# Patch loads of 16 rows plus two single rows, and patch writes issued on GpSimd, in a two-layer convolution by learned codes

## The chip, the cores and the metric

The kernel runs on one core of a Trainium2 chip. The metric is the device time of one execution in microseconds (us). A lower time is better.

## The reference, cut to what matters

The input is 16 images of 256 channels and 28x28 pixels. After a group norm, two layers of the same kind follow. In each, every channel's 3x3 patch (9 values) is compared with 16 codes; the softmax of the distances weights a table lookup, and the lookups are summed over channels.

```python
def amm_conv3x3(x, centroids, w_sub, stride=1):
    patches = jax.lax.conv_general_dilated_patches(x, (3, 3), (stride, stride), 'SAME')
    p = patches.reshape(B, C, s, Ho * Wo).transpose(0, 3, 1, 2)
    d = sum(p * p) - 2.0 * einsum('bncs,cks->bnck', p, centroids) + sum(centroids * centroids)
    attn = jax.nn.softmax(-d, axis=-1)                 # over the 16 codes
    lut = jnp.einsum('cks,cso->cko', centroids, w_sub)
    out = jnp.einsum('bnck,cko->bno', attn, lut)
    ...
# x + relu(se_layer(bn(amm(relu(bn(amm(gn(x))))))) + gn(x))
```

## The kernel before

The program is a plan of 32 stages (one layer of one image each) with 16 slots to a stage. A slot handles one unit: 32 channels and half of the pixels. From stage 2 to stage 28 the even stages are layer 2, and from stage 3 to stage 27 the odd ones are layer 1. Three kinds of transfers matter here, and they are issued by two engines.

```python
    def to_pat(l, i, pat, px=0, n=HW):          # patch WRITE, 12 per stage, used two stages later
        ...
        nc.scalar.dma_start(
            view(pat, (ROWS * p0 + 9 * k + 3 * dx) * HW + px, [[ROWS * HW, m], [HW, 3], [1, n]]),
            bass.AP(v.tensor, v.offset, [list(v.ap[0]), [W, 3], [1, n]]),
        )

    def patches(u, tile):                       # patch LOAD, four transfers of 18 rows
        ...
        for i in range(4):
            nc.sync.dma_start(
                pt[32 * i : 32 * i + ROWS, :, :n],
                view(u["pat"], (16 * u["m"] + i) * ROWS * HW + px, [[HW, ROWS], [4 * ROWS * HW, 4], [1, n]]),
            )

    def m_out(u):                               # maxima of a unit out to memory: two transfers
        for p0, n in ((0, P), (P, 96)):
            nc.scalar.dma_start(view(d, 32 * p0, [[32, n], [256 * 32, 4], [1, 32]]), u["mt"][:n])

    def m_in(u):                                # ... and back as extra rows of the patch tile: two transfers
        for j in range(NCH):
            nc.scalar.dma_start(u["pt"][MROW + j :: 32, :, :n], view(u["dm"], ...))
```

The round trip `m_out`, `m_in` through the buffer `dm` is made by two of the eight units in each pixel half of layer 2, so four times in a stage. The plan puts it behind an early pass of logits:

```python
                    if m in maxed:
                        a = s - self.lb                      # lb = 6 slots before the unit's own slot
                        self.loads.append((a - self.lead, s, u))   # lead = 3
                        at(a, MAX, a_logits, u)
                        ...
                        at(a + 2, TURN_BACK, m_turn, u)
                        at(a + 3, TURN, m_out, u)
                        at(a + 4, TURN, m_in, u)
                    else:
                        self.loads.append((s - self.lead, s, u))
                    at(s, LOGITS, b_logits, u)
                    at(s, EXP, b_exp, u)
    ...
    LOGITS, EXP, LOOK_A, NUM, TURN, SMALL, LOOK_B, MAX, LOOK_C, TURN_BACK, LOAD, REST = range(12)
```

## Time and profile before

| | before |
|---|---|
| time, median of 2 runs | 3104.32 us (3103.53 to 3105.12) |
| span of the profiled run | 3103.0 us |
| start to the first numerators | 54.8 us |
| stages 0 and 1 | 250.7 us |
| 13 layer-1 stages (3, 5, ..., 27) | 1257.8 us, mean 96.8 |
| 14 layer-2 stages (2, 4, ..., 28) | 1235.4 us, mean 88.2 |
| stages 29 to 31 and the end | 304.2 us |

A stage is timed from its first group of numerator matmuls to the first of the next stage, and a slot in the same way, so that a slot's time holds its own early logits (`a_logits`) and the next slot's logits (`b_logits`). The five rows of time add up to the span. The page of the profile has, further, the DMA queues (packets, megabytes, share of all 16 DMA engines' time) and the chain of work that ended last:

```profile
q10 hardware_dynamic: 151488, 244.45, 31.5%
q1 hardware_dynamic: 180560, 241.14, 30.6%
q0 software_dynamic: 6912, 38.54, 4.2%
PE 76%; DMA 10%; DVE 5%; POOL 3%; issue 2%; ACT 2%; ACTq 1%; SPq 0%; POOLq 0%; DVEq 0%
```

`q1` is SyncE's queue with the loads, `q10` is ScalarE's with the writes and the round trips, and `q0` is GpSimd's. The DMA engines are occupied for about two thirds of the span; a tenth of the last chain is transfers. TensorE carries three quarters of that chain.

### The profile page before, as it was taken

What the parts mean: (1) busy time and instruction counts of PE and PEld (TensorE: products, weight loads), DVE (VectorE), ACT (ScalarE), POOL (GpSimd) and SP (SyncE); (2) the same over time, 40 slices, a digit from 0 to 9 for tenths busy, and PEclk for the clock granted to TensorE, in tenths of its full rate; (3) what the DMA queues carried; (4) which work ended last, traced back from release to release, by engine and by line L of the source; (5) the groups of instructions that cost most, each with busy time, mean ns of one, the idle gap of its engine ahead of it and who ended that gap; (6) DMA issues with size and microseconds to landing.
All of it is one profiled execution on the core that took longest, in us unless ns stands there. A gap on an engine that the chain in (4) does not pass through costs nothing.

```text
span 3103.0 us, 94273 instructions
## 1 busy us (share of the span) xinstructions
PE 2966.8 (96%) x39834; PEld 1165.8 (38%) x39834; DVE 2254.3 (73%) x2760; ACT 1094.8 (35%) x1605; POOL 1506.4 (49%) x2163
## 2 busy tenths in 40 slices
PE   4998999999999999999999999999999999999997
PEld 3432333333333333333333333333333433334333
DVE  3464777777777777777777787777777777777785
ACT  2331342433434233342433334243343423333332
POOL 2352454555545455464545545455453545546444
PEclk8998999999999999999999999999999999999998
DMA  7866777767757676675767767676775767664552
GB/s 204 215 148 133 202 201 188 190 163 190 187 148 188 148 202 169 182 183 146 192 158 199 182 165 184 157 194 156 192 187 144 193 148 202 171 170 114 146 136 58
DMA packets 339391, 530.25 MB, mean 171 GB/s; under 512 B 94240, under 2 KB 265488, under 8 KB 338960
## 3 DMA queue, kind: packets, MB, share of 16 engines
q10 hardware_dynamic: 151488, 244.45, 31.5%
q1 hardware_dynamic: 180560, 241.14, 30.6%
q0 software_dynamic: 6912, 38.54, 4.2%
q8 instruction: 316, 5.18, 0.7%
q14 instruction: 115, 0.94, 0.1%
HBM read 269.96 MB, written 254.05 MB: 169 GB/s over the span
## 4 chain that ended last, share of the span: by engine, by line
PE 76%; DMA 10%; DVE 5%; POOL 3%; issue 2%; ACT 2%; ACTq 1%; SPq 0%; POOLq 0%; DVEq 0%
PE acc L695 45%; PE pair L631 15%; PE pair L563 15%; DMA pt<-pat 6%; DMA pat<-side 3%; DVE nt L643 2%; POOL k L659 1%; DVE rc L649 1%; ACT e L621 1%; DVE q L677 1%; POOL total L671 1%; DMA pat<-im 1%; ACTq L468 1%; PE pair L324 1%; DVE gn_st L417 0%
## 5 line engine op out<-in xcount | busy, mean ns | idle before, releaser
L695 PE MATMUL acc<-q,ws 128*128 128x384 f32 (+1 forms) x4096 | 1662.5, 525 | 5.3 <-ACT y L717 5.3
L659 POOL TENSOR_TENSOR k<-nt,rc 128x832 f32<-128x832 f32 (+1 forms) x512 | 804.8, 1572 | 1538.5 <-DVE rc L649 1527.1
L643 DVE STREAM_TRANSPOSE nt<-pair 128x832 f32<-128x832 f32 (+1 forms) x1024 | 977.4, 993 | 765.3 <-PE pair L631 640.7
L621 ACT ACTIVATE e<-pair 128x800 f32<-128x800 f32 (+1 forms) x1024 | 787.3, 821 | 1499.7 <-PE pair L563 1308.7
L695 PEld LDWEIGHTS acc<-q,ws 128*128 128x128 f32 x4096 | 705.1, 191 | 922.5 <-issue 610.0
L563 PE MATMUL pair<-pt,wd 19*32 19x384 f32 (+2 forms) x18432 | 626.5, 509 | 60.5 <-DMA pt<-pat 58.6
L631 PE MATMUL pair<-e,cw 32*32 32x384 f32 (+1 forms) x16384 | 585.9, 507 | 14.5 <-ACT e L621 13.3
L677 DVE STREAM_TRANSPOSE q<-k 128x832 f32<-128x832 f32 (+1 forms) x512 | 489.2, 956 | 0.8 <-POOL k L659 0.8
L649 DVE RECIPROCAL rc<-nt 128x104 f32<-128x104 f32 (+1 forms) x512 | 398.6, 779 | 17.6
L563 PEld LDWEIGHTS pair<-pt,wd 19*32 19x32 f32 (+1 forms) x18432 | 149.3, 103 | 440.6 <-issue 265.6
L631 PEld LDWEIGHTS pair<-e,cw 32*32 32x32 f32 x16384 | 167.2, 104 | 360.5 <-ACT e L621 317.9
L665 POOL TENSOR_TENSOR tail<-nt,rc 128x104 f32<-128x104 f32 (+1 forms) x512 | 245.1, 479 | 0.0
L695 PE MATMUL acc<-qt,ws 128*128 128x400 f32 (+1 forms) x512 | 218.8, 509 | 0.0
L671 POOL TENSOR_TENSOR total<-total,nt 128x96 f32<-128x96 f32 (+1 forms) x448 | 200.3, 447 | 0.0
L671 POOL TENSOR_TENSOR total<-total,rc 128x96 f32<-128x96 f32 (+1 forms) x448 | 179.1, 400 | 0.0
L695 PEld LDWEIGHTS acc<-qt,ws 128*128 128x128 f32 x512 | 91.0, 190 | 100.8 <-issue 51.3
L587 DVE TENSOR_REDUCE mx<-z 128x48 f32<-128x768 f32 (+1 forms) x128 | 120.8, 944 | 0.0
L582 DVE STREAM_TRANSPOSE z<-pair 128x768 f32<-128x768 f32 (+1 forms) x128 | 119.4, 971 | 1.8 <-PE pair L563 1.8
L707 ACT ACTIVATE im<-acc,bnsh,bnsc 128x384 f32<-128x384 f32 (+1 forms) x64 | 43.4, 678 | 137.0 <-PE acc L695 135.2
L717 ACT ACTIVATE y<-acc,bnsh,bnsc 128x384 f32<-128x384 f32 (+1 forms) x64 | 43.4, 679 | 88.7 <-PE acc L695 79.5
L525 DVE SCALAR_TENSOR_TENSOR y<-xt,gn_rstd,y 128x392 f32<-128x392 f32 x64 | 71.2, 1116 | 1.2 <-ACT y L519 1.2
L533 POOL TENSOR_TENSOR y<-y,xt 128x392 f32<-128x392 f32 x64 | 64.8, 1015 | 11.0 <-ACT y L529 11.0
(104 smaller groups left out, 620.7 us busy)
## 6 DMA issues: line engine op xcount, KB each, us to landing
pat<-side ACTq DMA_DIRECT2D x232, 588.0 KB
pt<-pat SPq DMA_DIRECT2D x1024, 112.5 KB
pt<-pat SPq DMA_DIRECT2D x1024, 108.0 KB
pat<-im ACTq DMA_DIRECT2D x116, 588.0 KB
xt<-in_x POOLq DMA_DIRECT2D x32, 784.0 KB, 8.7
out_dram<-y POOLq DMA_DIRECT2D x16, 784.0 KB, 6.4
pat<-side ACTq DMA_DIRECT2D x24, 300.0 KB
pat<-side ACTq DMA_DIRECT2D x24, 288.0 KB
```

Of the source, the lines that this page charges most:

```text
L563: nc.tensor.matmul(ps[t // 2][c : c + 32, t % 2, :n], lhsT=wd[l][32 * i : 32 * i + rows, 4 * u["m"] + t, :], rhs=u["pt"][32 * i : 32 * i + ...
L582: nc.vector.transpose(z[:, : 64 * nb].rearrange("p (t m) -> p t m", t=2), ps[:, :, : 32 * nb])
L587: nc.vector.tensor_reduce(u["mx"][:, 2 * v : 2 * v + 2].rearrange("p t (j b) -> p t b j", j=2)[:, :, :nb], u["z"].pop(0)[:, : 64 * nb].rea ...
L621: nc.scalar.activation(e[:, :, :n], ps[:, :, :n], AF.Exp, scale=2.0)
L631: nc.tensor.matmul(u["nm"][t // 2][32 * i : 32 * i + 32, t % 2, :n], lhsT=cw[l][c : c + 32, 4 * u["m"] + t, :], rhs=es[t // 2][c : c + 32, ...
L643: nc.vector.transpose(nt[:, :nb, 2 * v : 2 * v + 2].rearrange("p b t r -> p t b r"), ps[:, :, : 32 * nb].rearrange("p t (b r) -> p t b r", ...
L649: nc.vector.reciprocal(rc[:, : 8 * nb], u["nt"][:, :, SUM])
L659: nc.gpsimd.tensor_tensor(q[:, :nb].rearrange("p b (a s) -> p (b a) s", s=8), nt[:, :, :8], rc.unsqueeze(2).to_broadcast([P, 8 * nb, 8]), ...
L665: nc.gpsimd.tensor_tensor(tails[key][:, :nb, 8 * (m % 4) : 8 * (m % 4) + 8], nt[:, :, 8].rearrange("p (b a) -> p b a", a=8), rc.rearrange( ...
L671: nc.gpsimd.tensor_add(t[:, : 8 * nb], t[:, : 8 * nb], v)
L677: nc.vector.transpose(q[:, :, : 32 * nb].rearrange("p h (b r) -> p h b r", r=32), u.pop("k")[:, :nb].rearrange("p b (h r) -> p h b r", h=2),)
L695: nc.tensor.matmul(accs[key][:, :n], lhsT=ws[l][:, 2 * m + h if h < 2 else 2 * NQ + m // 4, o * P : (o + 1) * P], rhs=u["q"][h][:, :n], st ...
```

## The change

The intent is to have a load use all 16 DMA engines instead of nine, and to take the patch writes out of the way of the loads by another issuing engine. The load is also moved to an earlier place in each slot.

```diff
     def to_pat(l, i, pat, px=0, n=HW):
...
-        nc.scalar.dma_start(
+        nc.gpsimd.dma_start(
...
         for i in range(4):
             nc.sync.dma_start(
-                pt[32 * i : 32 * i + ROWS, :, :n],
-                view(u["pat"], (16 * u["m"] + i) * ROWS * HW + px, [[HW, ROWS], [4 * ROWS * HW, 4], [1, n]]),
+                pt[32 * i : 32 * i + 16, :, :n],
+                view(u["pat"], (16 * u["m"] + i) * ROWS * HW + px, [[HW, 16], [4 * ROWS * HW, 4], [1, n]]),
+            )
+        for r in range(16, ROWS):
+            nc.sync.dma_start(
+                pt[r::32, :, :n],
+                view(u["pat"], (16 * u["m"] * ROWS + r) * HW + px, [[ROWS * HW, 4], [4 * ROWS * HW, 4], [1, n]]),
             )
...
-    LOGITS, EXP, LOOK_A, NUM, TURN, SMALL, LOOK_B, MAX, LOOK_C, TURN_BACK, LOAD, REST = range(12)
+    LOGITS, LOAD, EXP, LOOK_A, NUM, TURN, SMALL, LOOK_B, MAX, LOOK_C, TURN_BACK, REST = range(12)
```

The matmuls and all arithmetic stay the same. A load has six transfers for four.

## The prediction

> **What bounds the kernel now.** I read the busy table first, then who TensorE (PE) waited for, then the same waits by stage, and last the queue of SyncE (SP), which issues the patch loads. The program is a row of 32 stages (layer 1 or layer 2 of one image) of 16 slots each. A slot is one unit: 16 small logits matmuls on a patch tile `pt` (L563), exp on ScalarE, 16 small numerator matmuls (L631), transposes, a scale on GpSimd, and some nine accumulating matmuls (L695).
>
> ```profile
> PE 2966.8 (96%) x39834; PEld 1165.8 (38%) x39834; DVE 2254.3 (73%) x2760; ACT 1094.8 (35%) x1605; POOL 1506.4 (49%) x2163
> PE pair L563 <- DMA pt<-pat: 58.6, 39, 4.9
> ```
>
> PE is busy 96%, so the whole idle time is 136 us, and nearly all of it in mid-program is the logits waiting for a patch load (58.6 us in 39 waits). Other engines are far from full. So the question is what these waits cost in all, and whether the change removes them. The stretches below are stage 15 (layer 1), stage 16 (layer 2) and stage 29 (the last layer-1 stage); columns are length, busy time of each engine (instructions), granted clock, DMA share, GB/s.
>
> ```profile
> 1506.80:1603.00 96.20, 92.48 (x1249) 35.62 (x1248) 69.09 (x82) 37.08 (x56) 51.12 (x77) 0.96 0.72 178
> 1603.00:1690.50 87.50, 87.50 (x1241) 34.62 (x1240) 70.76 (x88) 30.57 (x44) 42.61 (x60) 1.00 0.67 175
> 2798.80:2885.50 86.70, 86.70 (x1244) 34.55 (x1243) 69.24 (x82) 32.37 (x49) 49.55 (x70) 1.00 0.48 113
> ```
>
> A layer-1 stage takes 96.2 us, with 3.7 us of PE idle time and a mean clock of 0.96; a layer-2 stage has the same matmuls, no idle time, and takes 87.5. Stage 29 is a control that the program makes by itself: layer 1 again, but no patch writes beside it, since no later stage needs them; it takes 86.7. Taking slot by slot (start of one L631 group to the next), stage 15 loses all of it in slot 14: 15.3 us, against 7.8 in slot 14 of stage 29. The same slot takes 14.6 to 16.0 us in twelve of the thirteen layer-1 stages 3, 5, ..., 27 (11.1 in the other). In the timeline of PE it looks like this:
>
> ```profile
> 1585.46 0.93 PE L563 MATMUL pair<-pt,wd 19*32 19x384 f32 x32
> ...
> 1589.77 0.83 PE L563 MATMUL pair<-pt,wd 19*32 19x400 f32 x2 [1.84 <-DMA pt<-pat]
> 1591.79 3.41 PE L563 MATMUL pair<-pt,wd 19*32 19x400 f32 x30 [1.20 <-DMA pt<-pat]
> 1595.13 3.04 PE L695 MATMUL acc<-q,ws 128*128 128x400 f32 x4
> ```
>
> Two waits of 1.84 and 1.20 us; then 32 logits instructions take some 5.4 us where they took 0.93, as the row tiles land one by one; then four L695 matmuls take 3.04 us, normally 1.61. The clock records say why: half speed for 6.8 us from 1591.5. So a stall of 3 to 4 us costs 7 to 8. Over stages 2 to 30 I sum 55 us idle and 92 us at half clock.
>
> Why is the load late? SP's own queue:
>
> ```profile
> SPq L550 <- DMA pat<-side: 650.6, 180, 14.0
> SPq L550 <- DMA pat<-im: 404.4, 63, 15.1
> SPq L550 <- DMA pt<-pat: 378.1, 491, 4.6
> SPq L550 <- DMA dm<-mt: 304.6, 55, 21.4
> ```
>
> No load here reads a patch that is still being written: the writes (`pat<-side`, `pat<-im`, issued by ScalarE) are for a stage two later. The instruction records show the reason: loads and ScalarE's DMAs signal on the same eight semaphores in turn (108, 110 to 116), and SP waits for a semaphore's earlier transfer to land before using it again. At 1580.23 ScalarE issued a write on semaphore 115; the late load wanted 115 and was issued at 1586.70; SP had stood still since 1578.9. So 1055 us of SP's waits are false waits for patch writes.
>
> Second cause, the DMA engines. By packet size the trace has 150,624 load packets of 1536 or 1600 bytes, mean 96 ns, and about nine 4-byte completion packets per load (19,680 on that queue for some 2,150 DMAs). In stage 15, 9 or 10 load packets are in flight for 35 of 97 us and 11 or more for only 7: a load runs on nine engines.
>
> **What the Trainium skill says.** "DMA: Bandwidth & Descriptors", § Why a DMA increments its semaphore by 16 and not by 1: the number of engines is the largest k up to 16 that divides the slowest dimension of both sides. 18 rows give 9, which agrees with the trace; 16 rows would give 16, and the four-row transfers 4 (the lowest-numbered). The same page, § Issuing engines are not separate DMA queues: another issuer only saves issue time, so moving the writes to GpSimd frees no bandwidth; what I expect from it is the semaphores, which that section doesn't treat. § SWDGE vs HWDGE vs iDMA: GpSimd's descriptors are computed by software on its own cores. The trace: 0.75 to 0.81 us of GpSimd time per 256-row DMA, 0.58 us of queue time for ScalarE's. "TensorE: Matmul & The Clock Gate", Part 1: the clock falls to half after an idle window of about 3.4 us and needs a busy one to recover; the 6.8 us (two windows) agree.
>
> **The change part by part.**
>
> *Writes on GpSimd* (420 issues). GpSimd's DMAs use semaphores of their own (107 for its store), so SP's 1055 us of waits on writes go. Cost: 420 x 0.75 us (from the 0.75 to 0.81 of the larger `xt` and `out_dram` DMAs) = 315 us on GpSimd, 1506 to about 1820 us, 59%. It stands idle 1527 us waiting for `rc`; its result is used three slots later, so 0.75 us per slot lies beside other work. ScalarE loses 420 x 0.59 = 250 us of queue time, which is worth nothing to PE (13 us of waits for `e`).
>
> *16 + two single rows.* Engines 0 to 3 carry 16 + 8 = 24 packets per load, the rest 16, where nine carried 32. A layer-1 stage has 18 loads (two units' loads fall early): nine engines x 18 x 32 x 96 ns = 55 us each. Its other traffic: 0.72 x 16 x 96 = 1108 us of engine time, less 500 for loads (18 x 288 x 96 ns), over 16 = 38 us each. So those nine have 93 of 96 us full: layer 1 is bound by them too, and the lag builds up until slot 14. After: 18 x 24 x 96 ns = 41 + 38 = 79 us of 88 on four engines, 28 + 38 = 66 on the others. Tight, not full. Cost on SP: six issues for four, at 0.27 to 0.59 us (SP's range for shapes of this size): at most 3.5 us per 5.5 us slot.
>
> *Loads right behind the logits.* SP runs by itself, so this only changes whose semaphore a load gets in turn: it now stands before the slot's `dm` transfers. Worth 0 to 1 us per stage.
>
> Sum, stage by stage. Layer-1 stages 3 to 27 take 1257.8 us (13); with slot 14 at 7.5 and the other slots at their usual values one is 88.2, 1146.6 in all: 111 saved at most; I allow 1 us left in each: 98. Layer-2 stages 2 to 28 have 13 us over 14 x 87.3: 6 saved. Stage 30 (97.9, slot 6 takes 13.2 for about 7.3): 5. Stage 1 (125.9, loads behind small weight moves on SP, which stay): 8. Less 3 for unforeseen waits: 3104 - 114 = 2990 us.
>
> **Rivals.** (1) *The four single-row engines become the bound.* 79 of 88 us is an average; slot 11 has two loads, a patch write and the 784 KB store. If half the stall stays, PE may still idle a whole window: some 50 us saved, 3050. Against: SP can now run ahead by the spare tiles. (2) *The dm round trip takes its place.* ScalarE's `m_out` and `m_in` still share the eight semaphores, and SP waited 304.6 us on `dm<-mt`, 21 us at once. With six DMAs per load, eight semaphores span only 1.3 loads. But stage 30 and layer-2 stages have the same trips and mostly no stall, and `m_out` no longer queues behind writes: 3010 if it bites. (3) *GpSimd becomes late* by waiting in order for ScalarE's shifts, or by descriptor work: against it, 49% busy and three slots of slack; it would show 3060 or more. (4) *Everything hidden anyway*: against it, stage 29.
>
> **Range and chances.** The most that I can find is about 140 us (111 + 13 + 10 + some of stage 1), so 2962 is the low end; rival 1 in full gives the high end, 3045. The 2% line is 3042. Faster 0.85, same 0.12, slower 0.03.
>
> **What would show it.** PE's wait for `pt<-pat` falls from 58.6 us to under 15; layer-1 stages take 87 to 90 us, clock 1.00; SP's waits on `pat<-side` and `pat<-im` vanish; GpSimd gains 420 DMAs and some 300 us of busy time, without PE waiting on it; the load queue's share of the engines stays near 30%. I am wrong if slot 14 still takes over 11 us, if L695 starts to wait on `q`, or if a GpSimd-issued write slows the loads beside it.

## The result, and the profile after

The changed kernel takes 3491.82 us (3482.81 and 3500.82 in two runs), against 3104.32: a ratio of 1.1248, interval 1.1123 to 1.1374. It is slower by an eighth. A ratio is the mean time of one kernel's fast runs over the mean of the other's in the same rounds, so it is not quite the ratio of the two medians.

Line numbers move by six: the logits are now L569, the numerators L637, the lookup matmuls L701; the 16-row transfers are issued at L551 and the single rows at L556. The busy line of the changed kernel:

```profile
PE 3031.8 (87%) x39834; PEld 1185.9 (34%) x39834; DVE 2257.0 (65%) x2760; ACT 1096.5 (31%) x1605; POOL 1765.2 (50%) x2583
```

The instruction count of TensorE is the same, but it is busy 65 us longer (3031.8 for 2966.8) and idle 467 us (3498.9 - 3031.8) where it was 136. So 331 of the 396 us are idle time and 65 are matmuls at a lower clock. GpSimd has its 420 more instructions, and these cost what was foreseen:

```profile
L468 POOL DMA_DIRECT2D pat<-side x280 | 186.1, 665 | 5.1 <-DMA pt<-pat 4.3
L468 POOL DMA_DIRECT2D pat<-im x140 | 93.8, 670 | 2.7 <-ACT im L447 2.6
```

The columns are busy time, mean ns of one, and the idle time before: 280 us of issue, 0.67 us each. No wait of TensorE is for GpSimd's scale; one of 12.5 us, in the setup, is for GpSimd's squares (3.0 before). What TensorE does wait for (in all, times, longest):

```profile
PE pair L569 <- DMA pt<-pat: 265.8, 82, 7.4
PE pair L569 <- issue: 98.4, 22, 6.8
```

The wait that should have fallen from 58.6 us to under 15 rose to 265.8. (The second line is at the logits too. This view says "issue" where the last releaser came more than 1 us before the start; in 18 of the 22 waits that releaser was a load, `pt<-pat`, which had landed 1 to 3 us earlier. What held the logits from there on is not shown.) The chain that ended last has 52% TensorE for 76%, and 25% transfers for 10%:

```profile
PE 52%; DMA 25%; DVE 9%; issue 5%; POOL 4%; SPq 2%; ACT 1%; ACTq 1%; DVEq 0%; POOLq 0%
```

And the queue of SyncE, which issues the loads:

```profile
SPq L551 <- DMA dm<-mt: 436.3, 32, 17.6
SPq L556 <- DMA dm<-mt: 393.8, 44, 15.0
```

This is the view to compare with the one of before. The two lines for `pat<-side` and `pat<-im`, 1055 us together, are gone but for 15 us, as intended. In their place `dm<-mt`, which is `m_out`, went from 304.6 us to 436.3 + 393.8 = 830.1 us. No load reads `dm`; this is a false wait again, with another holder.

Where in the program the time went, stage by stage:

| | before | after | difference |
|---|---|---|---|
| start to the first numerators | 54.8 | 59.1 | +4.3 |
| stages 0 and 1 | 250.7 | 250.3 | -0.4 |
| 13 layer-1 stages | 1257.8 | 1294.7 | +36.9 |
| 14 layer-2 stages | 1235.4 | 1551.9 | +316.5 |
| stages 29 to 31 and the end | 304.2 | 343.0 | +38.8 |

Four fifths of the loss lie in the layer-2 stages, which by the prediction were to gain 6 us. Stage 15, stage 16 and stage 29 of the changed kernel answer to the three stretches that the prediction shows (length, busy time of each engine, granted clock, DMA share, GB/s):

```profile
1697.70:1797.50 99.80, 91.72 (x1245) 35.67 (x1244) 69.30 (x82) 37.05 (x56) 59.07 (x89) 0.93 0.78 175
1797.50:1906.30 108.80, 93.42 (x1237) 36.05 (x1236) 70.79 (x87) 30.79 (x44) 49.34 (x71) 0.92 0.65 137
3155.90:3247.50 91.60, 87.97 (x1243) 34.86 (x1242) 69.20 (x82) 32.32 (x49) 49.96 (x71) 0.98 0.56 115
```

Stage 16 takes 108.8 us for 87.5, with 15 us of idle TensorE where there was none, and the clock falls to 0.92. Stage 29, which has no patch write beside it (but for one in its first microsecond in the changed kernel, some 70 us before the stall) but does have the `m_out` of the stage behind it, went from 86.7 to 91.6, all of it in slot 14 (12.6 us for 7.8). That alone says that what is new does not need a patch write.

Slot by slot, the loss of the layer-2 stages sits in three places: slot 2 takes 11.6 us for 7.5, slot 6 takes 16.7 for 7.6, and slot 10 takes 12.9 for 4.8. In layer 1 slot 14 takes 18.4 for 14.8. These are the slots just behind an `m_out`. The timeline shows one of them, at the end of stage 15 (start, length, engine, and in brackets the idle time before and its releaser):

```profile
1770.00 1.91 ACTq L608 DMA_DIRECT2D dm<-mt  x2
...
1773.47 0.30 SPq L551 DMA_DIRECT2D pt<-pat  x1
...
1775.49 0.83 PE L701 MATMUL acc<-q,ws 128*128 128x400 f32 x2
1776.41 2.73 SPq L556 DMA_DIRECT2D pt<-pat  x2
1776.49 2.68 ACTq L614 DMA_DIRECT2D pt<-dm  x2
1779.24 2.07 SPq L551 DMA_DIRECT2D pt<-pat  x4
...
1782.39 1.60 PE L569 MATMUL pair<-pt,wd 19*32 19x384 f32 x32 [6.07 <-DMA pt<-pat]
```

ScalarE issues the two transfers of `m_out` from 1770.00 on. By the semaphore records they land at 1773.41 and 1776.40. SyncE issues one load transfer at 1773.47, on the semaphore of the first, and then stands still until 1776.41, when the second has landed and its semaphore is free. What is left of the load are the two single rows; the second takes 2.14 us to issue and lands at 1782.35. TensorE has run out of work at about 1776.3 and waits 6.07 us for the load. The 32 logits after it take 1.60 us instead of 0.93, since the granted clock is at half from 1778.7 on.

The theory from this, called A: SyncE's loads and ScalarE's transfers take turns on the same eight completion semaphores, and a transfer waits until the earlier one on its semaphore has landed. With the writes gone from ScalarE, the only other users are the round trips; and with six transfers to a load, eight semaphores come round faster, so that a load meets an `m_out` that has only just been issued. I counted this in the programs as built, where every transfer names its semaphore. In stages 3 to 27, this many load transfers have an `m_out` as the last user of their semaphore:

| | one slot ahead of the load's use | two slots | four slots | behind a patch write |
|---|---|---|---|---|
| before | 0 | 46 | 12 | 214 |
| after | 50 | 12 | 0 | 0 |

In the changed kernel the 50 are for the logits of slot 14 (26), 2 (12) and 6 (12), and the 12 at two slots are all for slot 11, whose logits lie in the time of slot 10: these are the four places that stall.

The turns are not those of the plan: a load that the plan places ahead of an `m_out` may take its turn behind it. They can be read off the built program all the same. In every one of these programs the transfers of SyncE and ScalarE together take the eight semaphores in strict rotation, in the order in which the built program lists them (2,835 transfers before, 3,439 after, none out of turn), and those of GpSimd take eight others in the same way. Why the build lists the transfers in that order I did not find out.

### The profile page after: what moved, and what is told of

The parts are those of the page before. It is cut to its first block, busy times and chain, and to the rows that moved or that the text cites.

```text
span 3498.9 us, 96490 instructions
## 1 busy us (share of the span) xinstructions
PE 3031.8 (87%) x39834; PEld 1185.9 (34%) x39834; DVE 2257.0 (65%) x2760; ACT 1096.5 (31%) x1605; POOL 1765.2 (50%) x2583
## 4 chain that ended last, share of the span: by engine, by line
PE 52%; DMA 25%; DVE 9%; issue 5%; POOL 4%; SPq 2%; ACT 1%; ACTq 1%; DVEq 0%; POOLq 0%
PE acc L701 30%; PE pair L637 11%; DMA pt<-pat 10%; PE pair L569 10%; DMA pt<-dm 5%; DMA dm<-mt 5%; DMA xt<-in_x 4%; DVE nt L649 3%; POOL k L665 2%; DVE q L683 1%; DVE rc L655 1%; SPq L556 1%; DVE mx L593 1%; DVE gn_st L417 1%; POOL total L677 1%
## 5 line engine op out<-in xcount | busy, mean ns | idle before, releaser
L701 PE MATMUL acc<-q,ws 128*128 128x384 f32 (+1 forms) x4096 | 1726.5, 542 | 5.3 <-ACT y L723 5.3
L701 PEld LDWEIGHTS acc<-q,ws 128*128 128x128 f32 x4096 | 728.2, 198 | 970.7 <-issue 679.0
L569 PE MATMUL pair<-pt,wd 19*32 19x384 f32 (+2 forms) x18432 | 601.8, 541 | 370.0 <-DMA pt<-pat 265.8
L637 PE MATMUL pair<-e,cw 32*32 32x384 f32 (+1 forms) x16384 | 582.5, 518 | 11.2 <-ACT e L627 9.5
L569 PEld LDWEIGHTS pair<-pt,wd 19*32 19x32 f32 (+1 forms) x18432 | 143.4, 106 | 723.1 <-issue 432.1
L637 PEld LDWEIGHTS pair<-e,cw 32*32 32x32 f32 x16384 | 162.7, 105 | 363.8 <-ACT e L627 296.3
L701 PE MATMUL acc<-qt,ws 128*128 128x400 f32 (+1 forms) x512 | 240.8, 555 | 0.0
L468 POOL DMA_DIRECT2D pat<-side x280 | 186.1, 665 | 5.1 <-DMA pt<-pat 4.3
L701 PEld LDWEIGHTS acc<-qt,ws 128*128 128x128 f32 x512 | 98.8, 206 | 115.9 <-issue 71.3
L468 POOL DMA_DIRECT2D pat<-im x140 | 93.8, 670 | 2.7 <-ACT im L447 2.6
```

Source lines behind the costliest of these rows:

```text
L468: nc.gpsimd.dma_start(view(pat, (ROWS * p0 + 9 * k + 3 * dx) * HW + px, [[ROWS * HW, m], [HW, 3], [1, n]]), bass.AP(v.tensor, v.offset, [l ...
L569: nc.tensor.matmul(ps[t // 2][c : c + 32, t % 2, :n], lhsT=wd[l][32 * i : 32 * i + rows, 4 * u["m"] + t, :], rhs=u["pt"][32 * i : 32 * i + ...
L637: nc.tensor.matmul(u["nm"][t // 2][32 * i : 32 * i + 32, t % 2, :n], lhsT=cw[l][c : c + 32, 4 * u["m"] + t, :], rhs=es[t // 2][c : c + 32, ...
L701: nc.tensor.matmul(accs[key][:, :n], lhsT=ws[l][:, 2 * m + h if h < 2 else 2 * NQ + m // 4, o * P : (o + 1) * P], rhs=u["q"][h][:, :n], st ...
```

## The experiments

All outputs are right. In the texts, A is the theory above, the one with the turns on the shared semaphores. The other letters are rivals, above all D, that the load or the number of DMA engines is the limit, and F, that the time at which the round trip is made decides and not the engine that issues it. Where a text counts "loads" behind an `m_out`, it counted load transfers. The three batches each had runs of the kernel before on the same chip: medians of 3105.46, 3106.15 and 3107.47 us, each of seven runs. Each experiment's time is the median of its runs. With 2% as the line, e1, e7, e8 and e11 count as the same as before and e3 as unclear; a smaller gain or loss is told below where the interval of the ratio leaves out 1.

All of them in one table (means in us over the stages named above; L1 is layer 1, L2 layer 2):

| | time | ratio | stages 0-1 | L1 stage | L2 stage | L1 slot 14 | L2 slots 2, 6, 10, 11 |
|---|---|---|---|---|---|---|---|
| before | 3104.32 | 1 | 250.7 | 96.8 | 88.2 | 14.8 | 7.5, 7.6, 4.8, 6.1 |
| after | 3491.82 | 1.1248 | 250.3 | 99.6 | 110.8 | 18.4 | 11.6, 16.7, 12.9, 5.8 |
| e1_writes | 3109.0 | 1.0003 | 223.4 | 97.0 | 90.1 | 15.8 | 7.8, 7.5, 5.1, 6.1 |
| e2_split | 3686.93 | 1.1871 | 280.5 | 115.9 | 107.0 | 16.0 | 11.1, 15.0, 11.0, 6.0 |
| e3_dm_pool | 3172.28 | 1.0208 | 256.4 | 90.6 | 97.0 | 7.9 | 7.3, 7.1, 4.8, 12.0 |
| e4_six18 | 3191.59 | 1.0275 | 229.8 | 97.2 | 94.6 | 15.8 | 8.3, 11.9, 5.2, 6.1 |
| e5_both_pool | 2961.7 | 0.9521 | 225.7 | 88.5 | 87.9 | 7.5 | 7.3, 7.1, 4.8, 6.1 |
| e6_both_pool_split | 3010.15 | 0.9679 | 249.3 | 88.9 | 88.3 | 7.9 | 7.3, 7.1, 4.8, 6.1 |
| e7_early | 3103.97 | 0.9981 | 253.1 | 96.9 | 88.2 | 15.0 | 7.5, 7.6, 4.8, 6.1 |
| e8_dm_pool_only | 3059.47 | 0.9843 | 246.5 | 93.8 | 88.0 | 11.1 | 7.3, 7.1, 4.8, 6.7 |
| e9_split_sooner | 3548.57 | 1.1421 | 262.8 | 101.3 | 110.9 | 13.6 | 7.7, 11.0, 6.6, 6.0 |
| e10_writes_sooner | 3338.65 | 1.0741 | 229.8 | 95.9 | 104.2 | 8.6 | 7.4, 7.1, 4.8, 6.1 |
| e11_both_pool_late | 3155.33 | 1.0152 | 219.3 | 91.3 | 97.3 | 7.5 | 7.3, 7.1, 4.8, 11.9 |

### e1_writes: only the writes on GpSimd

```diff
     def to_pat(...):
-        nc.scalar.dma_start(
+        nc.gpsimd.dma_start(
```

> Only the patch writes move to GpSimd; loads stay four transfers of 18 rows. Theory A (turns on eight shared semaphores): in the program as built, 62 of the loads in mid-program then take their semaphore from m_out two slots before their use (or more), and 13, one in each layer-1 stage, from m_out of the slot just before. So the stall in slot 14 of the layer-1 stages stays, with another cause (dm instead of a write), and the rest is undisturbed: 3060 to 3130 us. Theory B (the new shape of the loads is to blame, by the four engines that carry the single rows): this kernel keeps the old shape and loses the false waits for writes: about 3000 us. Theory C (a write issued by GpSimd slows the loads beside it): 3300 us or more.

Measured: 3109.0 us, ratio 1.0003 (0.9974 to 1.0031), the same. SyncE's waits are these:

```profile
SPq L550 <- DMA dm<-mt: 835.9, 79, 24.0
SPq L550 <- PE pair L563: 484.9, 300, 4.5
SPq L550 <- DMA pt<-pat: 403.7, 487, 4.1
```

The 1055 us on writes went but for 60.4 us, and 835.9 us on `m_out` came: the prediction's first cause was removed and gave nothing. Slot 14 still takes 15.8 us. In the built program 13 load transfers now stand one slot behind an `m_out`, all for slot 14 of layer 1; before there were none. Stages 0 and 1 gain 27 us, which the start (6 us later), the layer-2 stages and slot 14 give back.

### e2_split: only the shape of the load

```diff
-                pt[32 * i : 32 * i + ROWS, :, :n],
+                pt[32 * i : 32 * i + 16, :, :n],
...
+        for r in range(16, ROWS):
+            nc.sync.dma_start(pt[r::32, :, :n], ...)
```

> Only the loads change, to four transfers of 16 rows and two of 4; writes stay on ScalarE. Theory A: six transfers per load bring m_out to one slot before the load that reuses its semaphore in 37 of 49 places, and the waits for writes stay as well: 3400 to 3550 us. Theory B: slower too, since the shape is to blame, 3300 to 3500, but with loads that take longer from issue to landing, not with SP standing still for dm. Theory C (writes on GpSimd to blame): 3100 us or less.

Measured: 3686.93 us, ratio 1.1871 (1.1829 to 1.1913), slower than the whole change and above what A expected: the direction was right and the size was missed. Two queues' lines tell what it is:

```profile
PE pair L568 <- DMA pt<-pat: 443.7, 147, 8.1
```

```profile
SPq L555 <- DMA pat<-side: 446.1, 114, 13.7
SPq L555 <- DMA pat<-im: 256.3, 59, 9.1
SPq L550 <- DMA pat<-side: 221.5, 54, 13.8
```

With six transfers to a load and the writes still on the shared semaphores, loads queue behind writes as well as behind `m_out` (272 load transfers behind a write in the built program, 37 one slot behind an `m_out`). That shows in layer 1 too, outside the table: slots 5, 9 and 11 take 10.3, 12.5 and 10.8 us (5.5, 5.7 and 5.5 before), and 13, 26 and 13 load transfers for the logits of the next slots, 6, 10 and 12, stand behind a write. So the shape of the load is the part of the change that costs, and the move of the writes takes back some of it.

### e3_dm_pool: the changed kernel, with the round trips on GpSimd too

```diff
     def m_out(u):
-            nc.scalar.dma_start(...)
+            nc.gpsimd.dma_start(...)
     def m_in(u):
-            nc.scalar.dma_start(...)
+            nc.gpsimd.dma_start(...)
```

> The changed kernel with m_out and m_in issued by GpSimd too, so that only loads are left on the eight semaphores; shape and place of the loads as in the changed kernel. Theory A: the stalls in slots 14, 2, 6 and 10 go; 2980 to 3030 us, TensorE's wait for loads under 30 us. Theory B: the shape is still there, so is the time: over 3400 us. Theory C: the same, over 3400 us. What could spoil it under A: GpSimd stands still some 2 to 6 us per trip while m_in waits for m_out, at most 64 x 6 = 384 us of its idle time.

Measured: 3172.28 us, ratio 1.0208 (1.0178 to 1.0237). 320 of the 388 us come back (3491.82 to 3172.28), and the stalls in slots 14, 2, 6 and 10 are gone (7.9, 7.3, 7.1, 4.8). That supports A: the six-transfer load is the same, and only the partner on the semaphores was removed. But the time is well above the 2980 to 3030 expected, because a new wait came:

```profile
PE pair L568 <- DMA pt<-dm: 127.1, 61, 4.3
```

With GpSimd as the issuer `m_in` lands too late for the logits that need it, above all in slot 11 (12.0 us for 6.1), whose time holds the logits of slot 12, one of the four units with a round trip. The trace shows where the time goes: ScalarE has stood waiting for the maxima and issues `m_out` 0.03 us after they are ready (median of 64 trips, changed kernel); GpSimd, at the same place of the plan, issues it 5.49 us after. A sooner place brings that to 0.30 us (e6) and cures the wait.

### e4_six18: six transfers, but each of 18 rows

```diff
-        for i in range(4):
-            nc.sync.dma_start(pt[32 * i : 32 * i + ROWS, :, :n], ...)
+        for i in range(4):
+            for t0, nt in ((0, 2), (2, 2)) if i < 2 else ((0, 4),):
+                nc.sync.dma_start(pt[32 * i : 32 * i + ROWS, t0 : t0 + nt, :n], ...)
```

The writes are on GpSimd here, as in e1; the load runs on nine engines as before, but with six transfers.

> Writes on GpSimd; each load is six transfers of 18 rows (two row tiles cut in half by their four inner tiles), so the number of transfers is that of the changed kernel and the engines are the nine of the kernel before. Theory A: 26 loads take their semaphore from m_out of the slot before (13 in e1, 50 in the changed kernel): between e1 and the changed kernel, 3180 to 3350 us. Theory B: as e1, whatever that is, within 2%.

Measured: 3191.59 us, ratio 1.0275 (1.0242 to 1.0308). So the mere number of transfers costs 83 us over e1, with no change of engines. It is inside the range expected, but not where it was expected: slot 14 is unchanged (15.8) and the extra time is in slot 6 of layer 2 (11.9 for 7.5), whose time holds the logits of slot 7. The built program has 12 load transfers for slot 7 two slots behind an `m_out`, and e1 has just as many there without a stall (7.5 us); and for slot 14 it has 26 one slot behind where e1 has 13, at the same 15.8 us. The distance in slots alone therefore doesn't tell where a stall falls; that stays open.

### e5_both_pool: the kernel before, with writes and round trips on GpSimd, round trips sooner

```diff
     def to_pat(...), m_out(u), m_in(u):
-        nc.scalar.dma_start(
+        nc.gpsimd.dma_start(
...
-                        at(a + 3, TURN, m_out, u)
-                        at(a + 4, TURN, m_in, u)
+                        at(a + 2, REST, m_out, u)
+                        at(a + 3, REST, m_in, u)
```

> Writes and the dm transfers on GpSimd, loads four transfers of 18 rows, and m_out and m_in issued some half a slot to a slot sooner (end of slot a+2 and a+3 instead of middle of a+3 and a+4), because in e3 m_in came too late for its reader (127 us of waits of TensorE on pt<-dm). Theory A (only the turns on the eight semaphores held the loads back): no stall in slot 14, 2, 6 or 10; 2970 to 3010 us. Theory D (nine engines full, as in the prediction's second cause): the lag of the loads still builds up in layer-1 stages, slot 14 over 10 us there, 3040 us or more.

Measured: 2961.7 us, ratio 0.9521 (0.95 to 0.9543). This beats both kernels: 4.8% under before, 15% under the changed kernel (2961.7 / 3491.82 = 0.848, of two batches). Stages 15 and 16, who SyncE waits for, and TensorE's wait for the loads:

```profile
1432.00:1520.30 88.30, 87.72 (x1245) 34.66 (x1244) 69.25 (x82) 37.02 (x56) 61.90 (x93) 1.00 0.73 190
1520.30:1607.80 87.50, 87.50 (x1237) 34.61 (x1236) 70.75 (x87) 30.54 (x44) 57.32 (x82) 1.00 0.68 177
```

```profile
SPq L550 <- PE pair L563: 1418.6, 461, 6.4
...
SPq L550 <- DMA pat<-side: 93.5, 12, 12.7
```

```profile
PE pair L563 <- DMA pt<-pat: 5.1, 8, 1.7
```

Layer 1 now takes what layer 2 takes, at full clock. SyncE waits for what it should wait for: logits (`PE pair L563`) that free a patch tile. The 93.5 us on writes that are left are no false waits: writes and loads have no semaphore in common here. With the loads still on nine engines, the prediction's second cause, nine engines that are full, falls: slot 14 takes 7.5 us.

### e6_both_pool_split: e5 with the load of the change

This is the changed kernel (16 rows plus two single rows, load early, writes on GpSimd) with the two edits of e5 that it lacks: round trips on GpSimd, and sooner.

> As e5 but with the 16-row and single-row loads of the changed kernel. The difference to e5 is the shape of the loads alone, with nothing else on their semaphores. Theory A: within 1% of e5, 2970 to 3030 us. Theory B (four engines carry too much): over 1% slower than e5. Theory D: over 1% faster than e5.

Measured: 3010.15 us, ratio 0.9679 (0.9656 to 0.9702): better than before, but 1.6% behind e5, and so outside A's 1%. In the steady stages the two shapes are nearly equal: 88.9 and 88.3 us against 88.5 and 87.9, which makes 11 us in 27 stages. The larger part is in stages 0 and 1, 249.3 against 225.7. There TensorE waits 12.4 us for `part<-in_wsub` and 7.5 us for `ws<-dws`, moves of the weights in the setup, and for neither in e5. These moves share the semaphores with loads that take six turns; that this is why they are late I only argue. The load queue's line, with the queue's share of all engines, is

```profile
q1 hardware_dynamic: 198992, 241.21, 39.8%
```

against 31.2% in e5 for 180,560 packets and the same bytes. The 16 engines of a load do not make it cheaper: the same bytes hold more of the engines' time.

This run also settles a rival: that six transfers cost SyncE too much time to issue. The issues of the loads take 899 us in all before and 1856 in the changed kernel, but 1965 here, where the stalls are gone.

### e7_early: only the place of the load in the slot

```diff
-    LOGITS, EXP, LOOK_A, NUM, TURN, SMALL, LOOK_B, MAX, LOOK_C, TURN_BACK, LOAD, REST = range(12)
+    LOGITS, LOAD, EXP, LOOK_A, NUM, TURN, SMALL, LOOK_B, MAX, LOOK_C, TURN_BACK, REST = range(12)
```

> Only the place of the loads in the plan changes (right behind the logits). The program as built is the same instruction by instruction as the kernel before, names apart, so: the same time, 3104 us within 0.5%.

Measured: 3103.97 us, ratio 0.9981 (0.9952 to 1.001), the same. It could not be otherwise: the program as built is identical, instruction by instruction, with and without this line, names apart (34,385 instructions in the kernel before; 36,599 with the rest of the change). This part of the change does nothing.

### e8_dm_pool_only: round trips on GpSimd and sooner, writes left on ScalarE

```diff
     def m_out(u), m_in(u):
-            nc.scalar.dma_start(
+            nc.gpsimd.dma_start(
...
+                        at(a + 2, REST, m_out, u)      # was a + 3, TURN
+                        at(a + 3, REST, m_in, u)       # was a + 4, TURN
```

> Writes stay on ScalarE, loads stay as before, only the dm transfers go to GpSimd (sooner, as in e5). Theory A: the loads still take their semaphore from writes (224 of them), so slot 14 of the layer-1 stages still stalls: 3080 to 3130 us; either queue alone on GpSimd is worth nothing, both together some 100 us. Theory E (the dm trips were the whole cause in the kernel before too): 3000 us.

Measured: 3059.47 us, ratio 0.9843 (0.9817 to 0.9869). A expected 3080 to 3130, so this part is worth more alone than I thought. Slot 14 takes 11.1 us, halfway. SyncE's waits on writes are still there (777.1 us on `pat<-side`, 511.5 on `pat<-im`). The two holders of the semaphores thus each keep part of the stall. Taking away one gives 0 (e1) or 1.6% (e8); taking away both gives 4.8% (e5).

### e9_split_sooner and e10_writes_sooner: round trips sooner, but still on ScalarE

e9 is the changed kernel and e10 is e1, each with this edit alone:

```diff
-                        at(a + 3, TURN, m_out, u)
-                        at(a + 4, TURN, m_in, u)
+                        at(a + 2, REST, m_out, u)
+                        at(a + 3, REST, m_in, u)
```

> The changed kernel with m_out and m_in issued sooner, as in e5 and e6, but still by ScalarE on the eight shared semaphores. It separates the two edits that e5 and e6 made together. Theory A (the semaphores' turns): no better than the changed kernel, since 74 loads still take their semaphore from m_out one slot before: 3400 to 3600 us. Theory F (it was the sooner trip that helped in e6, not leaving the semaphores): near e6, 3050 us or less.

> e1 (writes on GpSimd, loads of 18 rows) with m_out and m_in sooner, still on ScalarE. Theory A: 26 loads one slot behind m_out and 48 two slots: as e1 or slower, 3100 to 3200 us. Theory F: near e5, 3000 us or less.

Measured: e9 3548.57 us, ratio 1.1421 (1.138 to 1.1461), inside its range; e10 3338.65 us, ratio 1.0741 (1.0713 to 1.077), above the 3100 to 3200 expected. Both refute F: the sooner trip alone makes either kernel worse. In e10 the loads are in time (11.0 us of waits for `pt<-pat`, 48.1 in e1; how much of that is the sooner trip and how much the longer stages is not shown), and yet it is slower than e1, by a wait that nobody had on the list:

```profile
PE pair L631 <- ACT e L621: 236.4, 80, 6.3
```

The numerators wait for the exp on ScalarE. At its sooner place `m_out` comes to its turn before its maxima (`mt`) are ready. ScalarE stands still until they are, and the exp behind `m_out` stands with it. One such place:

```profile
1720.47 0.31 DVE L595 STREAM_TRANSPOSE mt<-mx 128x128 f32<-128x128 f32 x1
1720.81 1.32 ACTq L602 DMA_DIRECT2D dm<-mt  x2
1722.24 1.51 ACT L621 ACTIVATE e<-pair 128x768 f32<-128x768 f32 x2 [7.47 <-issue]
...
1723.10 1.66 PE L631 MATMUL pair<-e,cw 32*32 32x384 f32 x32 [3.57 <-ACT e L621]
```

The maxima are there at 1720.78, `m_out` is issued at once, then comes the exp, and TensorE has been idle for 3.57 us. Over the run, ScalarE's exp waited 463.1 us, 62 times, for `mt`, and 42.5 us for `m_in`. In e9 the numerators' wait is 235.0 us, with another 138.6 for `pt<-pat`; so its time is right for partly another reason, and I can't say how it divides.

### e11_both_pool_late: e5 without the sooner round trips

```diff
     def to_pat(...), m_out(u), m_in(u):
-        nc.scalar.dma_start(
+        nc.gpsimd.dma_start(
```

> e5 without the sooner trip: writes and dm on GpSimd, m_out and m_in at their old places, loads of 18 rows. Theory A: loads are free (no stall in slot 14), but m_in comes too late for its reader as in e3, some 60 times 2 us: 3080 to 3140 us, with TensorE waiting 100 us or more on pt<-dm. If it were near e5, the sooner trip would not have been needed.

Measured: 3155.33 us, ratio 1.0152 (1.0125 to 1.018), a little above the 3080 to 3140 expected. Slot 14 is at 7.5 us, as in e5, so the semaphores alone remove that stall. But `m_in` is late, as in e3 (`m_out` is issued 5.53 us after its maxima), in slot 11:

```profile
PE pair L563 <- DMA pt<-dm: 144.3, 62, 5.5
```

GpSimd as the issuer and the sooner trip belong together. Either alone loses (e11, e10); together they gain.

## Why the prediction was wrong, point by point

**What bounds the kernel: right.** Slot 14 of layer 1 was lost to loads that wait on semaphores of other transfers, and 100 us and more were to be had. e5 has 107 us less in the 13 layer-1 stages (1257.8 to 1150.5) and 143 us less in all. The most that I foresaw, 2962, is by chance what e5 takes.

**"GpSimd's DMAs use semaphores of their own, so SP's 1055 us of waits on writes go": true, and the step that failed is to have booked it as gained time.** e1 does just this and has a ratio of 1.0003. The waits on writes were replaced by waits on `m_out`, 835.9 us in e1 and 830.1 after. A wait that ends last hides the one that would end next, and the sum of a queue's waits on one holder isn't what its removal is worth. Of the 502 us between the 2990 predicted and the 3491.82 measured, 119 are this gain that did not come (3109.0 in e1), and the other 383 came with the load of six transfers (e1 to the changed kernel, in two batches).

**Rival 2, the round trip: the right mechanism, put at 20 us over the prediction (3010 for 2990).** In the changed kernel it costs hundreds: 320 us come back with the round trips on GpSimd (e3), and 482 with that and the sooner trip (3491.82 to 3010.15, e6). I had written the cause, six transfers for eight semaphores, and argued it away with "stage 30 and layer-2 stages have the same trips and mostly no stall". That held only for four transfers to a load, with which no load stood one slot behind an `m_out`; with six, 50 of 62 do. The absence of a stall said nothing about a kernel with half as many transfers again. e4 shows the count alone at work, 83 us, and e2 the load's shape alone, 1.1871.

**The clock: right, and it multiplies.** The stall of the timeline idles TensorE for 6.07 us, and the matmuls behind it run slower: the lookup matmuls' mean went from 525 to 542 ns, and TensorE's busy time rose by 65 us. One detail is not as the prediction has it: the window before the fall was not idle throughout. The half clock began at 1591.5 before, with 0.83 us of matmuls in the 3.4 us ahead of it, and at 1778.7 after, 2.4 us after TensorE ran out of work.

**"Loads right behind the logits: worth 0 to 1 us": right in size, by a wrong working.** I reasoned that the load would stand before the slot's `dm` transfers. It does not: the built program is the same.

**Second cause, nine DMA engines 93 of 96 us full: wrong.** e5 keeps them and has no stall. The trace of before could have told: in 29.5 of the 96.2 us of stage 15 no load packet of 1536 or 1600 bytes was in flight. The packet count that I gave was right: 4-byte packets on the load queue went from 19,680 to 38,112. Less 1,248 of other transfers, they are 2048 x 9 before and 2048 x 16 + 1024 x 4 after, to the packet. But the load packets took 121 to 124 ns on average instead of 96. What I took for a lack of engine time was the false wait.

**GpSimd (rival 3): right to set it aside.** 420 issues cost 280 us (I said 315), beside other work; no wait of TensorE on it is among the long ones.

**The range.** Its high end was rival 1 alone, at 3045. Rival 2 had no tail, although it was the only rival in which the change itself makes a resource scarcer. It should have set the high end, and the chance of slower should have been far above 0.03.

**Still open:** why the build lists the transfers, and so gives out the turns, in that order; why e4 stalls in slot 6; what holds the logits at the end of the waits of the 98.4 us line in the changed kernel; how e9's loss divides; and why e6 loses 24 us against e5 in stages 0 and 1.

## What to carry to other kernels

When two engines' DMAs share a small set of completion semaphores, each transfer can wait for a stranger, so count the transfers between a load and the last slow user of its semaphore, before and after a change. To cut a load into more, better spread transfers shortens that distance. Before you book a removed wait as gain, ask which one ends next: here the two holders had to leave together, and the dependent transfer had to leave the queue of the engine that does other work, and start sooner, before anything was gained.

## What the Trainium skill lacked or had wrong

- "DMA: Bandwidth & Descriptors", § Issuing engines are not separate DMA queues, says that another issuer saves only the sequencer's time. For bandwidth no run here speaks against it, but it is not the only effect: in these programs the issuer decides which completion semaphores a transfer shares. Moving writes and round trips to GpSimd, with the trips made sooner, gave a ratio of 0.9521; the writes alone gave 1.0003.
- No page that I read tells of the cost of such a turn: loads waited 1055 us for patch writes that they did not read, then 830 us for `m_out` (304.6 before). A kernel author would need a warning that more transfers to a load bring the turn round sooner (e4: six for four, 1.0275 against 1.0003).
- "DMA: Bandwidth & Descriptors", § Rules for kernel authors, row "Use all 16 engines": here it bought nothing. With 16 and 4 engines for nine, but also six transfers for four, the layer-1 stages took 88.9 us against 88.5 and the kernel 3010.15 us against 2961.7 (e6, e5). What the page says on the number of engines agrees with the packets, exactly.
